# Four graph layers on one core: list keys by ScalarE and PE, and layer 0's row arithmetic moved between engines

## Chip, cores and metric

The kernel runs on one core of one Trainium2 chip. The metric is the device time of one execution in microseconds; lower is better. A profiled execution also gives a span, from its first to its last instruction, and the times inside it.

## What is computed

The input x holds 8 batches of 2048 nodes with 64 features, and adj a sparse 2048 x 2048 matrix of 0 and 1, the same for all batches. Four attention layers follow each other, each on the normalized and rectified rows, each added to x:

```python
h = jnp.maximum(_layernorm(x), 0.0); x = x + L0(h, adj)      # softmax(h h^T / 8, masked by adj) h
h = jnp.maximum(_layernorm(x), 0.0); x = x + L1(h, adj, W, a) # additive attention, elu
h = jnp.maximum(_layernorm(x), 0.0); x = x + L2(h, adj, ...)  # four heads, projection, second attention, layernorm
h = jnp.maximum(_layernorm(x), 0.0); x = x + L3(h, adj, W, a) # additive attention, relu
```

A node without neighbours takes the mean of all rows in layers 0, 1 and 3, since its masked softmax is uniform.

## The kernel before

**Layout.** Nodes lie in 16 tiles of 128 partitions; a row holds all batches, 8 x 64 = 512 float32 values (F). Attention is done edge by edge: for every tile the kernel makes lists of neighbour indices, gathers the neighbours' rows from a table in HBM into a ring of 26 slots in SBUF (`gather`, L260, one indirect DMA of POOL for each slot, 81 slots a layer), makes scores, weighs the rows and sums them on PE. A node's first few neighbours have slots of their own (`ROWS`); the rest of all nodes of a tile are packed into further slots (`PACKED`), which a selection matrix assigns to their nodes. Tile 0 holds the nodes with most neighbours and has 17 slots, the others 2 to 8.

**Stages.** `pipeline` runs a list of stage functions over the 16 tiles, each stage one tile behind the one before, the later stages first in each turn. That is the order in which the program is written down. A scheduler then reorders the instructions of each engine; an engine executes its own in the order that results. The first `pipeline` (set-up) loads x (`xin_rows`), normalizes it (`norm_a`, `norm_b`, `pre_c`) and stores the rows in table 0 (`pre_d`, `store_rows`). The second makes the lists (`load_adj`, `lists`), gathers from table 0 (`take0`), makes scores and their exponentials (`first0`), weights and sums (`second`), divides and adds to x (`third0`, `add_store`), normalizes again and stores table 1. Layer 1's gathers need all of table 1 and its mean row, and so on through tables 2, 3 (which have no mean row) and 4; table 4 is stored in the second half of layer 2 (after the four heads).

**Set-up of weights.** Before all this SP issues some 20 small transfers (L147 to L195), PE and VectorE form `u1`, `u3` and `q2` from them (L161 to L183, eight narrow copies to `q2`), and POOL issues three broadcasts of 64 values (L199) and seven of zero rows (L138, L140).

**Lists.** `load_adj` loads 128 x 2048 int32 values (L620). `lists` turns them into keys with one VectorE instruction over 2048 columns (L627): N + 1 minus the column where there is an edge, else 0. Then `max` (L633) finds the eight largest keys in each of 8, 16 or 22 segments of columns, for tile 0 twice with `match_replace` (L635) between; from these candidates `max` and `match_replace` (L643, L645) sort out the list, and narrow steps (L648 to L709) make indices, masks and the selection matrix, with small products on PE (L662, L685, L697) and the banks `q` and `m` in PSUM.

**Norms.** `norm_a` sums x on VectorE (L277). In set-up it does not centre: VectorE makes minus the mean (L289), ScalarE squares in eight pieces with it as bias (L291), POOL makes the product of mean and scale (L302), and ScalarE normalizes and rectifies in eight pieces (L308). In layer 0 it centres: VectorE makes the mean (L281) and subtracts it (L284), and ScalarE squares 512 columns at once (L285). `norm_b` sums the squares on VectorE (L297).

**Layer 0's end.** `third0` divides the sum `y` in PSUM on VectorE (L481) and `add_store` adds x to it there (L489).

**Mean row.** `store_rows` adds each tile's rows to `acc` on POOL (L367, L369; for tables 0, 1 and 4). After the last tile PE sums over partitions (L372), VectorE copies a row of 512 (L375) and SP stores it (L376).

**Products and sums.** `weigh_sum` multiplies two gathered rows at a time by their weights on POOL (L390) and sums them on PE (L395). L438 selects query rows on PE, L355 makes layer 1's per-node terms and L806 is the division of the four heads on ScalarE, in pieces of 64 columns.

Of the kernel before, what the change touches and what calls it, by code (L numbers as in the profile page):

```python
# [8 lines left out]
F32 = mybir.dt.float32  # L9
F16 = mybir.dt.float16  # L10
# [6 lines left out]
P = 128  # L17
# [14 lines left out]
SEGS = [(24, 2), (16, 1)] + [(8, 1)] * 14  # L32
RING = 26
# [5 lines left out]
SPREAD = 3  # L39

# [7 lines left out]
def segments(n, count, least):  # L48

    ends, lo = [], 0  # L50
    for k in range(1, count + 1):
        hi = n * k * k // (count * count)
        if hi - lo >= least:
            ends.append((lo, hi))
            lo = hi
    if lo < n:
        ends[-1] = (ends[-1][0], n)
    return ends
# [3 lines left out]
def edge_stack(ctx: ExitStack, tc: tile.TileContext, x_in, adj, w1, w1t, a1, wh, wht, bh, wo, bo,  # L62
# [47 lines left out]
    acc = const.tile([P, F], F32, name="acc")  # L110
# [28 lines left out]
    for k in (2, 3):  # L139
        nc.gpsimd.dma_start(out=table[k][N:N + 1, :], in_=zrow[:, :F])  # L140


    def diag2(name, src):

        t = const.tile([P, P], F32, name=name)
        nc.gpsimd.memset(t, 0.0)
        nc.sync.dma_start(out=t[:D, :D], in_=src)  # L147
        nc.sync.dma_start(out=t[D:, D:], in_=src)
        return t

    with tc.tile_pool(name="setup", bufs=1) as sp, \
            tc.tile_pool(name="ps_w", bufs=2, space=bass.MemoryType.PSUM) as ps_w:
        def attend_weights(name, wt, a):

            w2 = sp.tile([D, 2, D], F32, name="w2", bufs=2)
            nc.sync.dma_start(out=w2[:, 0, :], in_=wt)
            nc.sync.dma_start(out=w2[:, 1, :], in_=wt)
            av = sp.tile([D, 2], F32, name="av", bufs=2)
            nc.sync.dma_start(out=av, in_=a)
            p = ps_w.tile([P, D], F32, name="p")  # L160
            nc.tensor.matmul(p[:, :2], w2.rearrange("j t i -> j (t i)"), av, start=True, stop=True)  # L161
            u = const.tile([P, 4], F32, name=name)
# [3 lines left out]
            return u  # L166

        wd1, wd3 = diag2("wd1", w1), diag2("wd3", w3)
        u1, u3 = attend_weights("u1", w1t, a1), attend_weights("u3", w3t, a3)


        q2 = const.tile([P, 2, H, D], F32, name="q2")
        nc.gpsimd.memset(q2, 0.0)
        wh2 = sp.tile([D, H, 2, D], F32, name="wh2")
        for t in range(2):
            nc.sync.dma_start(out=wh2[:, :, t, :], in_=wh.rearrange("h d c -> d h c"))
        for h in range(H):
            p = ps_w.tile([P, D], F32, name="p")
            nc.tensor.matmul(p, wh2[:, h].rearrange("d t c -> d (t c)"), wh2[:, h, 0, :],
                             start=True, stop=True)  # L180
            for t in range(2):
                half = slice(t * D, (t + 1) * D)
                nc.vector.tensor_copy(q2[half, t, h, :], p[half, :])  # L183
    whd = [const.tile([P, P], F32, name=f"whd{k}") for k in range(2)]
    for k in range(2):
        nc.gpsimd.memset(whd[k], 0.0)
        for t in range(2):
            nc.sync.dma_start(out=whd[k][t * D:(t + 1) * D, t * D:(t + 1) * D], in_=wht[2 * k + t])
    bhc = const.tile([P, 2], F32, name="bhc")
    for k in range(2):  # L190
        nc.sync.dma_start(out=bhc[:, k:k + 1], in_=bh[k * P:(k + 1) * P].rearrange("(p o) -> p o", o=1))
    bhl = const.tile([P, 2], F32, name="bhl")
    nc.vector.tensor_scalar(bhl, bhc, SLOPE, None, op0=OP.mult)
    wo_sb = const.tile([P, 2, D], F32, name="wo")
    nc.sync.dma_start(out=wo_sb, in_=wo.rearrange("(k p) d -> p k d", p=P))  # L195

    def row_bcast(name, src, n):
        t = const.tile([P, n], F32, name=name)
        nc.gpsimd.dma_start(out=t, in_=bass.AP(tensor=src.tensor, offset=src.offset,  # L199
                                               ap=[[0, P], [1, n]]))  # L200
        return t

    bo_b = row_bcast("bo_b", bo, D)
    gamma_b = row_bcast("gamma_b", gamma, D)
    beta_b = row_bcast("beta_b", beta, D)


# [11 lines left out]
    def pipeline(*stages):  # L219

        states = {}
        for n in range(NT + len(stages) - 1):
            for s in reversed(range(len(stages))):
                if 0 <= n - s < NT:
                    i = order[n - s]
                    stages[s](i, states.setdefault(i, {}))
# [47 lines left out]
    def norm_a(src, st, centre):  # L274
# [4 lines left out]
        if centre:  # L279
            mean = tiny(B)  # L280
            nc.vector.tensor_scalar(mean, s, INV_D, None, op0=OP.mult)  # L281
            st["less"] = None
            st["src"] = rows_pool[0].tile([P, F], F32, name="ln_xc", bufs=3)
            nc.vector.tensor_tensor(heads(st["src"]), heads(src), wide(mean), op=OP.subtract)  # L284
# [38 lines left out]
    def pre_c(u):  # L323
        def f(i, st):
            st["xh"] = rows_pool[0].tile([P, F + B], F32, name="xh", bufs=3)
            scaled(st["xh"], st, AF.Relu)
# [35 lines left out]
    def store_rows(k, i, xh, mean):  # L362
        cols = table[k].shape[1]
        nc.sync.dma_start(out=table[k][i * P:(i + 1) * P, :], in_=xh[:, :cols])
        if mean:
            if i == order[0]:
                nc.gpsimd.tensor_copy(acc, xh[:, :F])  # L367
            else:
                nc.gpsimd.tensor_tensor(acc, acc, xh[:, :F], op=OP.add)  # L369
            if i == order[-1]:  # L370
                p = ps_m.tile([P, F], F32, name="m")
                nc.tensor.matmul(p[:1, :], ones, acc, start=True, stop=True)  # L372
                mr = rows_pool[0].tile([1, F + B], F32, name="mr", bufs=1)
                nc.vector.memset(mr[:, F:], 0.0)
# [108 lines left out]
    def third0(i, st):  # L483
        divide(st, st["y"])
        add_store(i, st, st["y"], True)
# [967 lines left out]
```

## Time and profile before

| | us |
|---|---|
| median of three runs | 1628.55 |
| the three runs | 1628.55, 1629.81, 1625.19 |
| the profiled execution's own time | 1627.04 |
| its span | 1625.3 |
| VectorE busy | 1289.1 (79%) |
| PE busy | 1209.7 (74%) |
| POOL busy | 1015.0 (62%) |
| ScalarE busy | 771.0 (47%) |
| first gather of layer 0 starts | 109.5 |
| first gather of layer 1 starts | 400.0 |
| first gather of layer 3 (table 4) starts | 1463.4 |

In a group's line the columns are: line, engine, operation, output and inputs, shapes, count; then busy time in us and mean ns of one; then the idle time of the engine just before these instructions, and what ended it. In a table by stretches each engine has its busy us and the number of its instructions. In a timeline a line begins with the start and the duration in us. DVE is VectorE, ACT ScalarE, POOL GpSimd, SP the engine that issues most DMAs; PEld is the load of weights into PE.

### The profile page before, as it was taken

To read this page: it belongs to the slowest core of one execution; us is meant where nothing else is said; L and a number is where in the kernel's file an instruction comes from. 1 tells how busy PE (TensorE), PEld (TensorE's weight loads), DVE (VectorE), ACT (ScalarE), POOL (GpSimd) and SP (SyncE) were. 2 spreads that over 40 slices of the span, in tenths; PEclk is the share of its full clock that TensorE was granted. 3 is DMA by queue.
4 is the path that set the end of the run, shared out by engine and by line. 5 is a ranking of instruction groups with operands and counts; after the bars stand their busy time and mean duration, and the time that the engine had idled before them with its cause. 6 is when DMAs were issued, how large, how long until landed. Compare 5 with 4: busy or idle time off the path is not lost. (4 is left out here: it accounts for less than half of the span.)

```text
span 1625.3 us, 15664 instructions
## 1 busy us (share of the span) xinstructions
PE 1209.7 (74%) x3771; PEld 607.8 (37%) x3771; DVE 1289.1 (79%) x2594; ACT 771.0 (47%) x2522; POOL 1015.0 (62%) x823
## 2 busy tenths in 40 slices
PE   0024766876799983699987999999766878855997
PEld 0012243444454531234343344443333334423555
DVE  6978999994689996899999699871159979954677
ACT  5861323444377882456532455555426446760011
POOL 4345865664763006898689889898276686527550
PEclk9999787787899997799999999999967987857899
DMA  5545555453787448566265344400084453227771
GB/s 177 179 152 190 179 189 174 142 186 122 225 289 264 155 160 309 203 207 211 66 223 185 121 151 170 164 13 7 30 313 139 125 168 120 79 79 218 214 211 61
DMA packets 85786, 266.93 MB, mean 164 GB/s; under 512 B 14627, under 2 KB 14659, under 8 KB 75446
## 3 DMA queue, kind: packets, MB, share of 16 engines
q0 software_dynamic: 37328, 141.05, 28.0%
q1 hardware_dynamic: 48358, 124.79, 21.8%
q8 instruction: 32, 0.52, 0.1%
q14 instruction: 68, 0.56, 0.1%
HBM read 208.74 MB, written 57.05 MB: 164 GB/s over the span
## 5 line engine op out<-in xcount | busy, mean ns | idle before, releaser
L260 POOL DMA_INDIRECT g<-table,idx x405 | 396.3, 978 | 234.2 <-issue 135.2
L783 POOL TENSOR_TENSOR wh<-g,w 128x1024 f32<-128x1024 f32 x162 | 307.3, 1918 | 35.6 <-PE y L798 33.6
L395 PE MATMUL y<-wg,ident 128*128 128x512 f32 x392 | 240.9, 744 | 50.2 <-POOL wg L390 44.2
L390 POOL TENSOR_TENSOR wg<-g,w 128x1024 f32<-128x1024 f32 (+1 forms) x91 | 155.1, 1717 | 74.8 <-ACT w L446 44.6
L770 DVE TENSOR_REDUCE s<-prod 128x32 f32<-128x2048 f32 x81 | 183.8, 2285 | 20.3 <-ACT w L772 19.9
L798 PE MATMUL y<-wh,ident 128*128 128x512 f32 x320 | 155.7, 614 | 22.7 <-POOL wh L796 20.6
L395 PE MATMUL y<-wg,selt 128*128 128x512 f32 x256 | 138.6, 651 | 8.7 <-POOL wg L390 8.1
L395 PEld LDWEIGHTS y<-wg,ident 128*128 128x128 f32 x392 | 83.2, 232 | 136.3 <-issue 67.4
L798 PE MATMUL y<-wh,selt 128*128 128x512 f32 x256 | 125.1, 614 | 12.1 <-POOL wh L783 12.1
L806 ACT ACTIVATE yn<-y,rec 128x64 f32<-128x64 f32 x512 | 111.3, 367 | 30.4 <-PE y L798 29.7
L369 POOL TENSOR_TENSOR acc<-acc,xh 128x512 f32<-128x512 f32 x45 | 58.0, 1288 | 96.8 <-ACT xh L308 84.6
L766 DVE TENSOR_TENSOR prod<-q,g 128x2048 f32<-128x2048 f32 x49 | 111.4, 2274 | 3.6 <-ACT g L764 3.3
L390 DVE TENSOR_TENSOR wg<-g,tiny 128x1024 f32<-128x1024 f32 (+1 forms) x92 | 98.2, 1085 | 11.6 <-PE y L395 11.2
L452 DVE SCALAR_TENSOR_TENSOR zt<-m,bhc,att 128x512 f32<-128x512 f32 x64 | 47.1, 736 | 75.3 <-ACT att L451 75.3
L438 PE MATMUL q<-rows,sel 128*128 128x512 f32 x128 | 84.3, 762 | 17.6 <-DVE prod L440 9.2
L798 PEld LDWEIGHTS y<-wh,ident 128*128 128x128 f32 x320 | 59.6, 195 | 96.9 <-issue 62.6
L409 PEld LDWEIGHTS m<-w,selt 128*128 128x128 f32 x384 | 62.6, 211 | 88.4 <-issue 26.2
L308 ACT ACTIVATE xh<-x,ln_r 128x64 f32<-128x64 f32 x256 | 88.3, 428 | 14.6 <-POOL ln_r L302 13.6
L409 PE MATMUL m<-w,selt 128*128 128x8 f32 (+1 forms) x384 | 59.7, 258 | 44.9 <-ACT w L555 17.2
L764 ACT COPY g<-g 128x512 f32<-128x512 f32 x81 | 50.4, 622 | 86.5 <-DVE prod L766 77.4
L790 PE MATMUL y<-rows,ident 128*128 128x512 f32 x128 | 70.2, 634 | 18.7 <-DVE prod L766 13.6
L766 DVE TENSOR_TENSOR prod<-qe,g 128x2048 f32<-128x2048 f32 x32 | 72.9, 2279 | 12.9 <-DMA qe<-qtab,qidx 11.7
(208 smaller groups left out, 2515.9 us busy)
## 6 DMA issues: line engine op xcount, KB each, us to landing
qtab<-q SPq DMA_DIRECT2D x16, 1040.0 KB, 4.3
a<-in_adj_dram SPq DMA_DIRECT2D x16, 1024.0 KB, 7.0
q<-qtab SPq DMA_DIRECT2D x14, 1040.0 KB, 6.3
table<-xh SPq DMA_DIRECT2D x48, 256.0 KB, 2.2
rows<-table SPq DMA_DIRECT2D x48, 256.0 KB, 3.6
xs<-x SPq DMA_DIRECT2D x48, 256.0 KB, 2.4
x<-xs SPq DMA_DIRECT2D x48, 256.0 KB, 4.6
table<-xh SPq DMA_DIRECT2D x32, 260.0 KB, 2.0
```

The costliest lines, as they stand in the source:

```text
L260: g = nc.gpsimd.indirect_dma_start(out=ring[:, (held[i] + t) % RING, :cols], out_offset=None, in_=table[k][:, :], in_offset=bass.IndirectO ...
L308: nc.scalar.activation(dst[:, b * D:(b + 1) * D], st["src"][:, b * D:(b + 1) * D], func, bias=0.0 if st["less"] is None else r[:, 1, b:b + ...
L390: eng.tensor_tensor(wg[:, :m].rearrange("p t (b d) -> p t b d", b=B), g[:, :, :F].rearrange("p t (b d) -> p t b d", b=B), w[:, t0:t0 + m, ...
L395: nc.tensor.matmul(y, lhs(i, t), wg[:, t - t0, :], start=(t == 0 and own is None), stop=(t == n - 1))
L409: nc.tensor.matmul(p[:, :cols], selt(i, t), packed[:, t, :], start=(t == 0), stop=(t == T - 1))
L438: nc.tensor.matmul(qe, sel(i, t - K), q, start=True, stop=True)
L766: nc.vector.tensor_tensor(pr.rearrange("p (b h) d -> p b h d", h=H), q[:, :B * H * D].rearrange("p (b h d) -> p b h d", h=H, d=D), heads(g ...
L770: nc.vector.tensor_reduce(s[:, t - lo, :], pr, AX.X, OP.add)
L783: nc.gpsimd.tensor_tensor(wg, heads(row(i, t))[:, :, None, :].to_broadcast([P, B, 2, D]), w[:, :, 2 * k:2 * k + 2, None].to_broadcast([P, ...
L790: nc.tensor.matmul(st["ys"][j], ident, xb[:, 4 * j:4 * j + 4], start=True, stop=False)
L798: nc.tensor.matmul(st["ys"][j], lhs(i, t), wg[:, 4 * j:4 * j + 4], start=False, stop=(t == n - 1))
L806: nc.scalar.activation(yn[:, b, h, :], st["ys"][j][:, b, h, :], AF.Copy, scale=st["rec"][:, 4 * j + b, 2 * k + h:2 * k + h + 1])
```

## The change

- Keys: ScalarE turns the int32 values into signs in bf16, in two halves of 1024 columns. PE makes each 512 columns of keys in PSUM from two bf16 products: 4096 times the sign, and the key N + 1 minus the column from two rows of small numbers that POOL makes once. Segments now end at multiples of 512. `max` and `match_replace` work in PSUM, and a narrow VectorE pass takes 4096 off the candidates, with zero as the floor.
- Layer 0: ScalarE divides in eight pieces, POOL adds x, makes the mean and centres.
- Set-up: POOL makes mean and centring, ScalarE squares 512 columns at once, VectorE rectifies and scales in one instruction.
- Mean row: for each tile PE sums 128 columns at a time over partitions, VectorE adds the 128 x 4 result to `acc`; at the end PE transposes it and SP stores 4 x 128 values.
- Weights are loaded by a function that is called where the fourth tile's adjacency is loaded, behind the first x tiles. The eight narrow copies to `q2` become two.
- Layer 0's stages get other distances (`LAG0`: the lists run three tiles further ahead of the gathers), lists and loads are written first in each turn, and PSUM has two `q` banks and two key banks in place of three `q` banks and a bank for small values.

```diff
+LIFT = 4096.0
+AHEAD0, LAG0 = (1, 0), [0, 1, 4, 5, 6, 7, 8, 9, 10]
...
 def segments(n, count, least):
+    marks = [n * k * k // (count * count) for k in range(1, count + 1)]
+    for at in range(512, n, 512):
+        near = min(range(count), key=lambda k: abs(marks[k] - at))
+        marks[near] = at
...
-    def pipeline(*stages):
+    def pipeline(*stages, ahead=(), lag=None):
...
-    def norm_a(src, st, centre):
+    def norm_a(src, st, centre, eng=nc.vector):
...
         if centre:
-            mean = tiny(B)
-            nc.vector.tensor_scalar(mean, s, INV_D, None, op0=OP.mult)
+            mean = tiny(B) if eng is nc.vector else small.tile([P, B], F32, name="ln_m")
+            eng.tensor_scalar(mean, s, INV_D, None, op0=OP.mult)
...
-            nc.vector.tensor_tensor(heads(st["src"]), heads(src), wide(mean), op=OP.subtract)
+            eng.tensor_tensor(heads(st["src"]), heads(src), wide(mean), op=OP.subtract)
...
-    def pre_c(u):
+    def pre_c(u, eng=None):
...
-            scaled(st["xh"], st, AF.Relu)
+            if eng is None:
+                scaled(st["xh"], st, AF.Relu)
+            else:
+                eng.scalar_tensor_tensor(heads(st["xh"][:, :F]), heads(st["src"]), 0.0,
+                                         wide(st["rstd"][:, 0, :]), op0=OP.max, op1=OP.mult)
...
         if mean:
+            C = F // P
+            p = ps_m.tile([P, F], F32, name="m")
+            for c in range(C):
+                nc.tensor.matmul(p[:, c:c + 1], xh[:, c * P:(c + 1) * P], ones, start=True, stop=True)
             if i == order[0]:
-                nc.gpsimd.tensor_copy(acc, xh[:, :F])
+                nc.vector.tensor_copy(acc, p[:, :C])
             else:
-                nc.gpsimd.tensor_tensor(acc, acc, xh[:, :F], op=OP.add)
+                nc.vector.tensor_tensor(acc, p[:, :C], acc, op=OP.add)
             if i == order[-1]:
                 p = ps_m.tile([P, F], F32, name="m")
-                nc.tensor.matmul(p[:1, :], ones, acc, start=True, stop=True)
-                mr = rows_pool[0].tile([1, F + B], F32, name="mr", bufs=1)
-                nc.vector.memset(mr[:, F:], 0.0)
-                nc.vector.tensor_copy(mr[:, :F], p[:1, :])
-                nc.sync.dma_start(out=table[k][N:N + 1, :], in_=mr[:, :cols])
+                nc.tensor.transpose(p[:C, :P], acc, ident)
+                mr = rows_pool[0].tile([C, P], F32, name="mr", bufs=1)
+                nc.vector.tensor_copy(mr, p[:C, :P])
+                nc.sync.dma_start(out=table[k][N, :F].rearrange("(c p) -> c p", p=P), in_=mr)
...
     def third0(i, st):
-        divide(st, st["y"])
-        add_store(i, st, st["y"], True)
+        y = rows_pool[0].tile([P, F], F32, name="att")
+        for b in range(B):
+            nc.scalar.activation(y[:, b * D:(b + 1) * D], st["y"][:, b * D:(b + 1) * D], AF.Copy,
+                                 scale=st["rec"][:, b:b + 1])
+        x = st["x"]
+        nc.gpsimd.tensor_tensor(x, x, y, op=OP.add)
+        nc.sync.dma_start(out=xs[i], in_=x)
+        norm_a(x, st, True, nc.gpsimd)
...
             def load_adj(i, st):
-                st["a"] = pool.tile([P, N], I32, name="a")
-                nc.sync.dma_start(out=st["a"], in_=adj[i * P:(i + 1) * P, :])
+                if i == order[WAT]:
+                    weights_in(pool)
+                st["e"] = pool.tile([P, N], BF16, name="e")
+                for c in range(0, N, N // 2):
+                    a = pool.tile([P, N // 2], I32, name="a")
+                    nc.sync.dma_start(out=a, in_=adj[i * P:(i + 1) * P, c:c + N // 2])
+                    nc.scalar.activation(st["e"][:, c:c + N // 2], a, AF.Sign)
...
-                key = st["a"].bitcast(F32)
-                nc.vector.scalar_tensor_tensor(key, st["a"], 0.0, keyrow, op0=OP.is_gt, op1=OP.mult)
...
+                for c in range(0, N, F):
+                    key = ps_k.tile([P, F], F32, name="k")
+                    nc.tensor.matmul(key, lift, st["e"][:, c:c + F], start=True, stop=False)
+                    nc.tensor.matmul(key, every, keys[:, c:c + F], start=False, stop=True)
...
+                ends = c1.rearrange("p s r k -> p (s r k)")
+                nc.vector.tensor_scalar(ends, ends, LIFT, 0.0, op0=OP.subtract, op1=OP.max)
...
-            pipeline(xin_rows, lambda i, st: norm_a(st["x"], st, False), pre_b, pre_c(None), pre_d(0, None))
+            pipeline(xin_rows, lambda i, st: norm_a(st["x"], st, True, nc.gpsimd), pre_b,
+                     pre_c(None, nc.vector), pre_d(0, None))
             pipeline(load_adj, lists, take0, both(first0, xin_rows), second, third0, pre_b, pre_c(u1),
-                     pre_d(1, u1))
+                     pre_d(1, u1), ahead=AHEAD0, lag=LAG0)
```

`weights_in` issues the transfers, memsets, products and copies that stood at the program's start, and the three broadcasts of POOL.

## Prediction

> **What bounds the kernel now.** I read the busy time by stage first: the share over the whole span hides that only the first quarter is changed. The stages are cut at three places of POOL's timeline: the first landed x (16.6 us), the first gather of layer 0 (109.5) and the first gather of layer 1 (400.0).
>
> ```profile
> core 0: us, PE busy (x) PEld busy (x) DVE busy (x) ACT busy (x) POOL busy (x), PEclk, DMA share, GB/s
> 0.00:16.60 16.60, 3.47 (x12) 2.91 (x12) 3.12 (x16) 1.28 (x1) 11.02 (x35) 1.00 0.37 63
> 16.60:109.50 92.90, 3.50 (x9) 1.62 (x9) 78.09 (x260) 79.71 (x298) 29.58 (x33) 1.00 0.52 179
> 109.50:400.00 290.50, 199.15 (x607) 107.72 (x607) 260.58 (x795) 106.53 (x377) 184.27 (x143) 0.83 0.52 172
> ```
>
> VectorE works 78 of 93 us in set-up, where ScalarE is as full (80), and 261 of 290 us in layer 0; between 140 and 360 us most stretches of 10 us show it at 8.4 to 10.0. So VectorE bounds the first 400 us, and its work there is what an edit can shorten. Next, the groups of 16.6 to 400 us by shape, to see what the edited lines cost:
>
> ```profile
> L627 DVE SCALAR_TENSOR_TENSOR a<-a,keyrow 128x2048 f32<-128x2048 int32 x16 | 38.2, 2390 | 7.7 <-DMA a<-in_adj_dram 7.7
> ...
> L481 DVE TENSOR_TENSOR y<-y,rec 128x512 f32<-128x512 f32 x16 | 11.0, 689 | 0.5 <-PE y L395 0.5
> L489 DVE SCALAR_TENSOR_TENSOR x<-y,x 128x512 f32<-128x512 f32 x16 | 10.9, 681 | 0.1
> L284 DVE TENSOR_TENSOR ln_xc<-x,tiny 128x512 f32<-128x512 f32 x16 | 10.8, 676 | 0.1
> ```
>
> The last column is small in all of these: VectorE hardly waits before them. The same groups on POOL, which will take up work:
>
> ```profile
> L260 POOL DMA_INDIRECT g<-table,idx x82 | 87.5, 1067 | 51.5 <-issue 31.9 <-DVE idx L708 7.2 <-DVE junk L659 4.7
> L390 POOL TENSOR_TENSOR wg<-g,w 128x1024 f32<-128x1024 f32 x36 | 68.5, 1906 | 34.6 <-ACT w L446 16.8 <-PE y L395 9.1 <-issue 6.5
> L369 POOL TENSOR_TENSOR acc<-acc,xh 128x512 f32<-128x512 f32 x30 | 38.9, 1298 | 51.0 <-ACT xh L308 42.4 <-ACT xh L358 2.7 <-DVE c L645 1.6
> L390 POOL TENSOR_TENSOR wg<-g,w 128x512 f32<-128x512 f32 x9 | 9.4, 1044 | 5.4 <-ACT w L446 5.4
> ```
>
> Last, the timeline at the end of layer 0, where the mean row is what layer 1 waits for:
>
> ```profile
> 391.70 1.27 POOL L369 TENSOR_TENSOR acc<-acc,xh 128x512 f32<-128x512 f32 x1 [1.75 <-ACT xh L308]
> ...
> 395.23 1.86 PE L372 MATMUL m<-acc,ones 128*1 128x512 f32 x2
> ...
> 397.13 0.68 DVE L375 COPY mr<-m 1x512 f32<-1x512 f32 x1 [8.82 <-PE m L372]
> 397.84 0.24 SPq L376 DMA_DIRECT2D table<-mr  x1
> 399.97 0.98 POOL L260 DMA_INDIRECT g<-table,idx  x1 [7.01 <-issue]
> ```
>
> **What the Trainium skill says.** "GPSIMD Engine Reference", section 1, has its SBUF interface shared with VectorE, with contention against VectorE instructions that have two SBUF inputs or a 2-port mode. The trace agrees: a pair of 128x8 products on POOL (L302, usually 0.20 us each) takes 2.33 us at 45.59 us, while L627 runs on VectorE. Section 4.1 calls two-input elementwise work about 2x slower there; here 128x512 takes 1.27 us (L369) against 0.68 (L489). "TensorE: Matmul & The Clock Gate", part 1, halves the clock after an idle window; the table above shows 0.83 granted in layer 0.
>
> **The change, part by part.** Durations are of the profiled execution: span 1625.3 us, its own time 1627.0, 1.5 below the median of 1628.55.
>
> *Off VectorE:* L627 38.2; division, addition, centring 11.0 + 10.9 + 10.8; the means L281 and L289 2.5 + 4.2; set-up's copies L183 1.8 less 0.7; two mean-row copies 1.4. Together 80 us. *Onto VectorE:* set-up's rectify-and-scale as one 128x512 instruction per tile, 16 x 0.68 = 10.9 (price of L489); removing the lift from the candidates, 16 narrow passes, 3.5 by their widths; 32 mean-row additions of 128x4 at 0.15 (as L666), 4.8; and 194 searches and replacements that now read PSUM. The nearest rows, one element from PSUM and from SBUF, are 144 ns (L666) and 133 (L663): 194 x 11 = 2 us; "VectorE: DVE Perf Modes", errata section, puts 62 cycles between the two, at its 0.96 GHz 65 ns, 12.6 us; I take 3. Sum 22. Net: 341.8 - 80 + 22 = 284 us of VectorE work. It is on the path, as VectorE bounds.
>
> *Earlier start:* x is now issued first, weights later. VectorE starts at about 5 us (one issue of 0.6, landing 2 to 4) and not at 16.6. The 20 weight transfers of 0.33 to 0.6 us each now stand on SP among list loads and ahead of the seventh x; six loaded x and the lists cover their 11 us, which is the price if they don't. The three on POOL (1.9 us) stand between the first means and the first centring; POOL's memsets, iotas (two key rows, some 1.9 each like L598) and nine zero-row issues take 15.5 us before that.
>
> *ScalarE:* loses L291 (32.5) and set-up's L308 (43.5); gains 16 squares of 0.627 (10.0), 32 signs of 128x1024 and layer 0's division as 128 pieces at 111.3/512 = 0.217 each (L806), 28. A sign has no row: "ScalarE: Activation LUTs" prices 186 + 0.833 N ns, 1.04 us; the slope of L679 (364 ns at 128 columns, 692 at 512) gives 1.13. I take 1.04, 33 us in all, 36 at the upper end. About even at 187 us; covered by VectorE and POOL.
>
> *PE:* gains 128 bf16 key products of 512 columns. A float32 one is two instructions, 0.43 us each at full clock; bf16 lies between 0.22 ("VectorE: DVE Perf Modes", 6 + N cycles at 2.4 GHz) and 0.43: I take 0.25 with weights, 32 us (28 to 55). The mean rows are eight small instructions per tile as at L355, some 0.9 us, 16 tiles a table. Layer 0's PE need at full clock is 143 us now (81 sums of 2 x 0.43, 70; 32 selections 28; the small ones 45) and 176 then (72 late keys 19, mean rows 14): inside the window found below, but no longer slack.
>
> *POOL:* loses L369 and L367 (41 us in these stages). Set-up gains 16 centrings of 1.04 (L390) to 1.27 (L369), taken as 1.16, and 16 means of 0.2: 22 us. Layer 0 gains the same and 16 additions of 1.27: 42 us.
>
> *New waits:* division on ScalarE, addition, mean and centring on POOL form a loop through POOL's queue, where each add waits for ScalarE and each mean for VectorE, with gathers and products queued behind. The key products wait on PE behind sums that wait for POOL, with two key banks and two instead of three q banks; lists run three tiles further ahead to cover it.
>
> **The sum for layer 1's first gather.** The built order of the changed kernel puts 26 gathers, tile 0's 17 slots among them, before POOL's first product; the last need tile 0's list. Ahead of its end stand on VectorE, counted in that order: norms 16 x (0.60 + 0.60 + 0.60 + 0.15) = 31 us; tile 0's own list 34 (44 searches and 22 replacements by segment 12.5, 31 passes over 352 candidates at 0.5, small steps); five other lists and one search 33. That is 98, and 5% for stalls in small steps, since the same count of the kernel before gives 323 where 341.8 is busy: 103 us. From 5 us at 93% that ends at 116 us. POOL then has 55 gathers at 0.95 + 0.30 spacing (69), products 68.5 + 9.4 (78) and 42: 189 us. VectorE has 284 - 103 = 181. POOL is now the longer. Layer 2 (700 to 1100 us), where POOL is 347.5 us busy of 400, shows the share a leading POOL reaches: 87%. 189/0.87 = 217, so 333. From the last centring to the gather about 10 us (square 0.6, ln_q 0.6, ln and exp 0.5, xh 2.0, transposes and copy 1.2, L355 0.9, copies 0.3, store 2.0, issues the rest): 343 instead of 400.0, so 57 saved.
>
> *Layer 3:* the stage that makes its table (1200 to 1463 us) drops 20 us of POOL adds, next to VectorE's 227 of 263 us, for 14 us of PE. At the end the mean row no longer follows 1.86 us of products and a 0.68 us copy; table rows stored at 1459.1, landing 2.0 later, are late next: 2 to 3 of the gap to 1463.4 go. I take 3 for the stage, zero to 6. The other stages keep their order nearly whole: 0. Total 1627.0 - 60 = 1567 in the profiled scale, about 1568 against the median; I write 1567.
>
> **Rivals.** *Both queues fill:* if VectorE and POOL overlap as VectorE alone did before (97%), 112 + 189/0.97 + 10 = 317: 83 + 3 saved, 1541. For: L627's blocking of POOL is gone, some 11 us. Against: two full engines wait on each other. *Coupling takes it:* POOL reaches only what it had from 172 to 392 us, 144 busy + 16 of issue gaps of 220, 73%: 116 + 259 + 10 = 385, 1609. For: waits of 2 to 5 us before products in the trace. Against: VectorE, which caused them, has slack. *Slower:* the POOL loop. 48 added waits per layer (add, mean, centre, 16 tiles); the sum without idleness is 116 + 189 + 10 = 315, so it decides from (403 - 315)/48 = 1.8 us each. At 2.3 us, near the waits of 2.8 seen before L369, it is 425 and, less 3, 1649. Against: the order puts other work between. *The change does nothing:* freed time is only waited through, 1627.
>
> **How the numbers follow.** Forecast 0.55, both full 0.15, coupling 0.17, POOL loop 0.10, nothing 0.03. Faster by over 0.3% (about what a measurement of this kernel can tell from no change) is the first three, less a corner of coupling: 0.86; same 0.03; slower 0.11. The range 1535 to 1617 leaves out the slower case, the unchanged one and the outer parts of coupling and of both full; the forecast's own is 1545 to 1590.
>
> **What would show it.** First gather of layer 0 near 60 us; POOL's 26th gather at 105 to 125; layer 1's first at 320 to 365; VectorE's sum to there near 284; L627's 38 us gone; table-end gaps shorter by 2 to 3 us. It is wrong if POOL's idle time before the moved adds and centrings passes 1.8 us each, if PE is busy throughout layer 0, or if later stages move by over 10 us.

## The result, and the profile after

The changed kernel takes 1599.64 us (median of 4 runs, 1596.62 to 1602.38) against 1626.87 for the kernel before beside it: ratio 0.983, 95% interval 0.980 to 0.986, 27 us less. Repeated on another chip the ratio was 0.982 (0.978 to 0.985). The forecast was 60 us less. The profiled execution took 1597.0 us, its span is 1595.3, so the profiles differ by 30 us (1625.3 before).

Busy time of the changed kernel by stage, cut at layer 0's first gather, at POOL's first product, after the last centring and at layer 1's first gather:

```profile
core 0: us, PE busy (x) PEld busy (x) DVE busy (x) ACT busy (x) POOL busy (x), PEclk, DMA share, GB/s
0.00:77.50 77.50, 46.28 (x164) 31.80 (x165) 53.35 (x196) 29.93 (x68) 37.55 (x73) 1.00 0.74 227
77.50:139.30 61.80, 38.76 (x112) 18.50 (x111) 55.43 (x289) 19.00 (x40) 24.67 (x26) 0.92 0.60 193
139.30:353.70 214.40, 189.46 (x694) 104.73 (x694) 185.00 (x542) 127.57 (x473) 170.22 (x148) 0.86 0.54 173
353.70:367.30 13.60, 9.68 (x44) 8.72 (x43) 1.45 (x5) 4.58 (x17) 0.02 (x2) 0.50 0.21 78
```

Layer 0's first gather comes 32 us earlier than before (77.5 against 109.5), but POOL's first product does not: 139.3 against 133.7. From there to layer 1's first gather it is 228 us instead of 266, and this is the gain that is left: 367.3 against 400.0. After that 1228 us follow, 3 more than before. Two places of VectorE's and POOL's timelines in set-up show what became of the early start (in brackets: idle time before, and what ended it):

```profile
8.35 0.17 DVE L621 TENSOR_SCALAR nn<-pe 128x16 f32<-128x16 f32 x1
21.85 0.83 DVE L191 TENSOR_SCALAR bhl<-bhc 128x2 f32<-128x2 f32 x1 [13.34 <-DMA bhc<-in_bh_dram]
22.59 0.67 DVE L267 TENSOR_REDUCE ln_s<-x 128x8 f32<-128x512 f32 x1
```

```profile
101.30 0.95 POOL L250 DMA_INDIRECT g<-table,idx  x1 [0.30 <-issue]
129.60 0.94 POOL L250 DMA_INDIRECT g<-table,idx  x1 [27.34 <-DVE mbb L692]
```

A 128x2 step for layer 2's bias stands eighth among VectorE's instructions, and its transfer (bhc) stands on SP behind list loads: VectorE's bulk begins at 21.9 us. POOL waits 27 us for the rest of tile 0's list, and eight gathers at 1.25 us follow before its first product.

The end of layer 0 in the changed kernel:

```profile
362.28 1.84 PE L363 MATMUL m<-ones,xh 128*128 128x1 f32 x8
...
364.16 0.16 DVE L367 TENSOR_TENSOR acc<-m,acc 128x4 f32<-128x4 f32 x1 [5.05 <-PE m L363]
...
364.88 0.28 DVE L372 COPY mr<-m 4x128 f32<-4x128 f32 x1 [0.56 <-PE m L370]
365.19 0.27 SPq L373 DMA_DIRECT2D table<-mr  x1
367.29 1.03 POOL L250 DMA_INDIRECT g<-table,idx  x1 [13.58 <-DMA table<-mr]
```

The mean row is still last. Its eight products take 1.84 us here, where the clock on record is 0.50, and 0.95 to 1.04 in the dense stretch from 320 to 345 us, where it is 1.00.

Next, the stretch of VectorE's bulk, from its start to where the last scores are done, before (first fence) and after:

```profile
16.60:378.00 361.40, 187.42 (x559) 100.02 (x560) 329.64 (x1036) 174.70 (x631) 207.35 (x170) 0.88 0.53 178
```

```profile
21.80:340.00 318.20, 260.95 (x903) 146.02 (x904) 287.00 (x1008) 159.09 (x524) 204.36 (x191) 0.89 0.59 190
```

VectorE is as full as before (90% against 91%), with 43 us less of work in 43 us less of time. POOL is at 64%. What has changed is PE: 52% before, 82% after.

### The profile page after: what moved, and what is told of

It is laid out like the page before. It is cut to its first block, busy times and chain, and to the rows that moved or that the text cites. A ratio compares the mean times of both kernels' runs of the same rounds, so it can differ in the third digit from the quotient of the medians.

```text
span 1595.3 us, 16704 instructions
## 1 busy us (share of the span) xinstructions
PE 1293.1 (81%) x4280; PEld 672.1 (42%) x4280; DVE 1245.6 (78%) x2569; ACT 762.7 (48%) x2443; POOL 1002.1 (63%) x844
## 4 chain that ended last, share of the span: by engine, by line
PE 34%; DVE 17%; POOL 10%; ACT 10%; issue 9%; DMA 7%; SPq 0%; POOLq 0%; DVEq 0%; ACTq 0%
PE y L392 9%; PE y L820 9%; POOL g L250 5%; DMA g<-table,idx 4%; DVE prod L788 3%; DVE s L792 3%; POOL wh L805 3%; ACT yn L828 2%; DMA rows<-table 2%; ACT xh L298 2%; PE y L812 2%; PE m L869 2%; PE m L857 2%; PE q L435 2%; DVE wg L387 2%
## 5 line engine op out<-in xcount | busy, mean ns | idle before, releaser
L250 POOL DMA_INDIRECT g<-table,idx x405 | 386.8, 955 | 290.2 <-issue 111.1
L392 PE MATMUL y<-wg,ident 128*128 128x512 f32 x392 | 225.7, 705 | 19.5 <-POOL wg L387 11.7
L392 PE MATMUL y<-wg,selt 128*128 128x512 f32 x256 | 131.0, 621 | 2.3 <-POOL wg L387 2.3
L392 PEld LDWEIGHTS y<-wg,ident 128*128 128x128 f32 x392 | 79.5, 222 | 97.6 <-issue 62.1
L435 PE MATMUL q<-rows,sel 128*128 128x512 f32 x128 | 80.8, 730 | 9.1 <-DVE prod L437 7.4
L333 PE MATMUL q<-q,xt 128*128 128x512 f32 x128 | 67.3, 635 | 18.3 <-DVE prod L335 10.4
L363 PE MATMUL m<-ones,xh 128*128 128x1 f32 x384 | 68.8, 302 | 10.4 <-DVE idx L729 3.5
```

The lines of the kernel that those rows point to most:

```text
L250: g = nc.gpsimd.indirect_dma_start(out=ring[:, (held[i] + t) % RING, :cols], out_offset=None, in_=table[k][:, :], in_offset=bass.IndirectO ...
L363: nc.tensor.matmul(p[:, c:c + 1], xh[:, c * P:(c + 1) * P], ones, start=True, stop=True)
L392: nc.tensor.matmul(y, lhs(i, t), wg[:, t - t0, :], start=(t == 0 and own is None), stop=(t == n - 1))
L435: nc.tensor.matmul(qe, sel(i, t - K), q, start=True, stop=True)
```

## The experiments

Theory 1, the blocked start: the early list work is what counts, and the wait for bhc takes it away. Theory 2: when VectorE starts matters little, since tile 0's list and what follows set the rest. Theory 3: the mean row costs more on PE than on POOL. Theory 4, formed after the first runs: POOL's start-up work holds the front. Ratios are to the kernel before on the same chip: on some chips it takes 1627 us, on others 1673 to 1675. The difference lies behind layer 1's first gather. This is layer 1's stage of the changed kernel in the first profile and in its repetition:

```profile
367.30:587.90 220.60, 183.62 (x662) 98.19 (x662) 177.32 (x342) 146.64 (x426) 80.20 (x97) 0.93 0.63 211
```

```profile
368.10:610.30 242.20, 185.70 (x662) 99.23 (x662) 177.25 (x342) 146.67 (x426) 80.16 (x98) 0.89 0.58 192
```

The same work on each engine takes 22 us longer where the DMA engines move 192 GB/s instead of 211; up to 367 us the two profiles agree within 1 us. So stages are compared only up to layer 1's first gather, and times as ratios. 0.001 of the time before is 1.6 us.

One thing limits most of these runs: the scheduler orders each edited program anew. How much of the changed kernel's order is left was counted in the traces, up to layer 1's first gather, as the longest sequence that both have in common. With the bias first, with table 4's mean row on POOL and in the first two runs on the end of the tables, at least 1021 of VectorE's 1029 instructions keep their order. In the other edited runs it is 569 to 940, so they weigh their edit together with a new order. Layer 1's first gather comes at 362 to 368.5 us in the first group and at 369 to 405 in the second: the order may itself be worth several us, and no run tries it apart.

In the line after each run: ratio (interval); layer 0's first gather, POOL's first product, layer 1's first gather in us.

**The changed kernel again**, with no edit.

> The changed kernel as it is, for a profile on the same chip as the three runs with added work. All theories: ratio 0.983 within 0.003; first product at 139, layer 1's first gather at 367 within 5 us.

Measured: 0.9816 (0.9781 to 0.9850); 77.5, 140.2, 368.2. It repeats.

**The bias first.** The two transfers of bhc and the step on them at the head of the program:

```
-            nc.sync.dma_start(out=bhc[:, k:k + 1], ...)      # in weights_in
-        nc.vector.tensor_scalar(bhl, bhc, SLOPE, None, op0=OP.mult)
+    for k in range(2):                                       # ahead of weights_in
+        nc.sync.dma_start(out=bhc[:, k:k + 1], ...)
+    nc.vector.tensor_scalar(bhl, bhc, SLOPE, None, op0=OP.mult)
```

> The changed kernel with the two bias transfers issued first and the 128x2 product of bhl behind them, so that no wait of 13.3 us on VectorE is left; all else in its order. Theory 1 (the early list work on VectorE sets the time, and the wait for bhc at 8.5 to 21.9 us takes it away): VectorE works through 10 to 20 us, the last of the first 26 gathers ends near 129 instead of 139.3, layer 1's first gather comes near 357 instead of 367.3, time near 1588 (10 less than the changed kernel). Theory 2 (the lists' first rows, x behind them on SP and tile 0's chain of small steps set it, whenever VectorE starts): the idle time only moves to waits for x, keys or PE, layer 1's first gather within 3 us of 367, time 1595 to 1600.

Measured: 0.9819 (0.9795 to 0.9844); 75.2, 137.9, 365.8. The 13 us wait is gone and 1.5 to 2.4 us come of it. Nearly all else keeps its order (1026 of VectorE's 1029 instructions). VectorE's timeline of this run shows the next wait in its place:

```profile
16.97 0.69 DVE L269 TENSOR_REDUCE ln_s<-x 128x8 f32<-128x512 f32 x1 [8.60 <-POOL ln_m L273]
```

The first means stand on POOL behind its memsets, key rows and issues. The blocked start is real, but as the explanation of the missing time it falls.

**POOL's start-up too.** The bias first, and the nine zero-row and three broadcast transfers issued by ScalarE:

```
-        nc.gpsimd.dma_start(out=table[k][N + 1:N + 2, :], in_=zrow[:, :table[k].shape[1]])
+        nc.scalar.dma_start(out=table[k][N + 1:N + 2, :], in_=zrow[:, :table[k].shape[1]])
```

> The kernel with the bias first, and besides POOL's nine zero-row transfers and three broadcast transfers (together 6.9 us of POOL's first 22) issued by ScalarE, so that the key rows and the first centring come some 6 us earlier. Theory 4 (what ends the start-up is POOL: its memsets, iotas and issues stand ahead of the first centring at 19.8 us and of the keys, and VectorE has little to do before): the first gather of layer 0 comes near 70 instead of 75.2, tile 0's list at 124 instead of 128.2, the ratio to before 0.979. Theory 2 (tile 0's list and what follows set it): 129 at the earliest, ratio as that of the run with the bias first, 0.982.

Measured: 0.9859 (0.9825 to 0.9894); 71.0, 138.8, 383.5. The first gather moves as expected; the first product does not move at all, and the end of layer 0 comes later. VectorE is busy for only 10.4 of the 20 us from 80 to 100, with gaps of 3.4 and 3.2 us, ahead of a weights' copy and a key search, whose cause the trace doesn't name. Theory 4 finds no support; it isn't refuted, as the order is new and the twelve transfers now stand in ScalarE's queue.

**Tile 0 first** in the order of making:

```
-MAKING = [15, 14, 13, 0, 12, 11, 10, 1, 9, 2, 8, 3, 7, 4, 6, 5]
+MAKING = [0, 15, 14, 13, 12, 11, 10, 1, 9, 2, 8, 3, 7, 4, 6, 5]
```

> The changed kernel with tile 0, whose list of 17 slots takes VectorE 34 us, first in the order in which lists and table rows are made, not fourth; all else as changed. If POOL's wait of 27 us for tile 0's list at 102 to 130 us (and its eight gathers, 9.7 us, behind it) is what took the gain, products start near 110 instead of 139 and layer 1's first gather comes 15 to 20 us earlier: ratio 0.972. If VectorE's total work sets the time, whatever its order, or POOL's stretch only grows: ratio within 0.003 of the changed kernel's 0.983.

Measured: 0.9847 (0.9817 to 0.9877); 77.2, 133.5, 377.4.

**No lists ahead:**

```
-                     pre_d(1, u1), ahead=AHEAD0, lag=LAG0)
+                     pre_d(1, u1))
```

> The changed kernel with layer 0's stages one turn apart in the old order (no lists ahead). If lists that run three tiles ahead keep the first scores, and so POOL's first product, waiting until 139 us, the first product comes near 105 and the time falls by up to 15 us: ratio 0.974. If the lead covers the key products' waits on PE behind sums, as the prediction had it, VectorE waits for keys in layer 0: ratio 0.990 to 1.000.

Measured: 0.9832 (0.9788 to 0.9875); 77.3, 88.8, 379.4. The first product comes 50 us earlier and the kernel is no faster. With the last two runs this speaks against POOL's late first product as what the end of layer 0 hangs on. It doesn't show it, since these edits change the order of all engines too, and this one takes away the lists' lead.

**Weights first**, `weights_in(pool)` called ahead of both pipelines:

> The changed kernel with its weights' transfers and small products called ahead of the two pipelines, as the kernel before had them; all else as changed. If the later weights are what brings the earlier start (as the prediction had it, 11 us of transfers on SP), x comes some 10 us later and the time rises by about 10, to 1610. Theory 1: the changed kernel loses those 10 us anyway, to bhl's wait and to x behind weights and lists; the time stays within 4 us of the changed kernel's, near 1600, or falls a little below it.

Measured: 0.9866 (0.9845 to 0.9888); 83.4, 144.6, 383.8. It lies between the two: 6 us later at the first gather and some 7 us in the time. The later weights, with the order that comes with them, are worth that.

**Work added in layer 0, read by nobody**, to see which engine holds it. One edit each, behind the added x (VectorE, POOL) and in the mean row of table 1 (PE):

```
+        nc.vector.tensor_reduce(spare, heads(x), AX.X, OP.add)         # 16 x 0.68 us
+        nc.gpsimd.tensor_tensor(spare, x, x, op=OP.add)                # 16 x 1.27 us
+                    nc.tensor.matmul(p[:, C + c:C + c + 1], xh[:, c * P:(c + 1) * P], ones, ...)
```

> The changed kernel with one more reduction of 128x512 per tile on VectorE in layer 0, behind the added x: 16 x 0.68 = 10.9 us more of its work, read by nobody. If VectorE still bounds the first stages (it starts its bulk at 22 us, has 295 us of work and a drain of some 22 us behind its last bulk), the time rises by 10 to 12 us, ratio 0.990. If POOL bounds layer 0, as the prediction had it, by less than 3: ratio 0.983 to 0.985.

Measured: 0.9866 (0.9830 to 0.9902); 75.9, 139.7, 387.1. Against the repetition, which ran on the same chip, it is 8 us for 10.9, and all four times lie above all four of that run. Layer 1's first gather comes 19 us later; the same code behind it then takes 1265.9 us, against 1276.9 in the repetition, and why is open.

> The changed kernel with one more POOL addition of 128x512 per tile in layer 0, behind the added x: 16 x 1.27 = 20 us more of its work, read by nobody. If POOL bounds layer 0 (the prediction's sum: 189 us of work at 87%), the time rises by 20 us or more, ratio 0.996. If VectorE bounds it, by less than 5: ratio 0.983 to 0.986. If both are coupled through their waits, in between.

Measured: 0.9819 (0.9783 to 0.9854); 77.8, 141.2, 374.6. On the same chip again, there is no loss in the time for 20 us of POOL work (6 us at layer 1's first gather in this one profile).

> The changed kernel with the small products of table 1's mean row done twice: 64 more products of 128x1 and weights, 0.95 to 1.84 us per tile, 15 to 29 us of PE's time in layer 0, read by nobody. If PE has slack in layer 0 (189 of 214 us busy, at 0.86 of the clock), the time rises by no more than the tail's 1.8 us: ratio 0.983 to 0.985. If PE's in-order queue bounds it, by 15 us and more: ratio 0.993.

Measured: 0.9896 (0.9852 to 0.9940); 76.7, 140.1, 379.8. Some 10 us, with a wide interval that just touches the changed kernel's; all four times lie above those of the repetition. So the runs suggest that POOL has room and that VectorE and PE have little. They don't show it, for the order is new in each: with the POOL work, for instance, VectorE keeps 905 of 1029 instructions in order, PE 888 of 1010 and ScalarE 491 of 597, though nothing was added to these.

**Less VectorE work**: the lift removed by ScalarE.

```
-                nc.vector.tensor_scalar(ends, ends, LIFT, 0.0, op0=OP.subtract, op1=OP.max)
+                nc.scalar.activation(ends, ends, AF.Relu, bias=unlift)
```

> The changed kernel with the removal of the lift (16 steps of 128x64 to 128x352, 8.9 us of VectorE, of which 6 are waiting inside the instruction) on ScalarE, as one rectify with a bias. If VectorE's work sets the first 340 us, they shorten by 6 to 10 us: ratio 0.977. If the round trip through ScalarE's queue costs each list its own wait: ratio 0.982 to 0.988.

Measured: 0.9809 (0.9783 to 0.9834); 76.9, 140.6, 369.1. VectorE has 275 us of work from 21.8 to 340 instead of 287, and next to nothing comes of it. Either VectorE does not hold the stretch alone, or the way through ScalarE's queue and the new order (745 of 1029 kept) cost as much as was saved; this run can't tell.

**Parts undone.** Layer 0's division, addition, mean and centring back on VectorE (`divide(st, st["y"])` and `add_store(i, st, st["y"], True)` in `third0`):

> The changed kernel with layer 0's division, addition, mean and centring back on VectorE (32.6 us there, 42 us off POOL, 28 off ScalarE). The prediction's sum (POOL leads layer 0 with 189 us, VectorE has 181): the balance turns, VectorE has 214 and POOL 147, the stretch after the first product grows by some 10 us, ratio 0.989. Rival (the move was what made POOL the longer and gained nothing): ratio 0.978 to 0.983.

Measured: 0.9939 (0.9910 to 0.9969); 76.8, 140.3, 383.2. This part, with its order, is worth some 19 us.

Set-up's norm back on ScalarE:

```
-            pipeline(xin_rows, lambda i, st: norm_a(st["x"], st, True, nc.gpsimd), pre_b,
-                     pre_c(None, nc.vector), pre_d(0, None))
+            pipeline(xin_rows, lambda i, st: norm_a(st["x"], st, False), pre_b, pre_c(None), pre_d(0, None))
```

> The changed kernel with set-up's norm as before: means folded into ScalarE's squares (32.5 us) and its rectify (43.5 us), nothing of it on POOL, 11.3 us of rectify off VectorE. If set-up is held by VectorE and the wait for x and lists, ScalarE's 76 us fit beside them and the time stays within 5 us: ratio 0.980 to 0.986. If ScalarE's signs (33 us over lists) wait behind these, set-up ends near 105 us as before and the time rises by 15 to 25 us: ratio 0.993 to 0.999.

Measured: 0.9893 (0.9869 to 0.9918); 107.2, 150.6, 378.8. Set-up ends 30 us later, as before the change, but the kernel loses only some 11 us.

The mean rows back on POOL, in tables 0, 1 and 4, then in table 4 alone:

```
+            if i == order[0]:
+                nc.gpsimd.tensor_copy(wide_acc, xh[:, :F])
+            else:
+                nc.gpsimd.tensor_tensor(wide_acc, wide_acc, xh[:, :F], op=OP.add)
```

> The changed kernel with the mean row of tables 0, 1 and 4 added on POOL and closed by one PE product of 128x1 by 128x512, as before; all else as changed. Theory 3 (the small fp32 products on PE, 1.84 us a tile at half clock, cost more than POOL's 1.26 us adds): layer 0's first gather comes some 3 us earlier, the tail of layer 0 shortens by 3, layer 3's stage by 4; time near 1590. Rival (POOL leads layer 0, so 16 adds of 1.26 us lengthen it): 139 to 354 us grows by about 20 us, against 7 gained at the ends; time near 1612.

Measured: 0.9954 (0.9937 to 0.9971); 86.8, 151.7, 394.4.

> The changed kernel with the mean row of table 4 alone added on POOL as before. Theory 3: layer 3's stage loses the 4.6 us by which it grew, time near 1595 (4 to 5 less than the changed kernel). Rival (the growth there comes from elsewhere, such as the two transfers into the table's last row, or is spread by chance of the order): within 2 us of the changed kernel, 1598 to 1602.

Measured: 0.9800 (0.9776 to 0.9823); 77.5, 141.2, 368.5. The first costs some 20 us, so theory 3 finds no support for the whole of the mean rows. Want of POOL time is hardly the reason in layer 0, as the run with added POOL work suggests; in set-up, where 9 of the 20 us are lost, no such run was made. These adds wait for a finished row, with gathers and products queued behind, which fits but was not tried apart. In table 4 alone it makes no difference that can be told.

All three parts undone, which leaves keys by sign and PE, later weights and lists ahead:

> The change cut down to its keys by ScalarE's sign and PE, the later weights and the lists three turns ahead: set-up's norm back on ScalarE with its rectify, layer 0's division, addition, mean and centring on VectorE, the mean rows on POOL as before. VectorE's law (its work over 0.90 of the time between its start and its end): 295 + 33 in layer 0 and, in set-up, +4 for the means, less 11.3 for the rectify, 4.5 for mean rows, so 316 us of work against 295, some 23 us later than the changed kernel, ratio 0.997. If POOL bounds the changed kernel's layer 0, giving it back 62 us of adds and centrings shortens it: ratio 0.975.

Measured: 1.0062 (1.0041 to 1.0083); 111.3, 168.2, 405.4. Alone they make the kernel 10 us slower, although VectorE has 23 us less to do up to layer 1 (319 against 342). Which of the three does it, or whether the order does, was not tried apart. The three parts are worth some 50 us one by one and some 40 together, so they overlap.

**The end of the tables.** The mean row of the last five tiles of tables 1 and 4 by VectorE, from the transposed tile that is there anyway:

```
+            late = k in (1, 4) and i in order[-5:]
+            if late:
...
+                nc.vector.tensor_reduce(col, xt, AX.X, OP.add)
+                nc.vector.scalar_tensor_tensor(acc, col, 1.0 / N, acc, op0=OP.mult, op1=OP.add)
```

> The changed kernel, but the mean row of the last five tiles of tables 1 and 4 is summed by VectorE from the transposed row tile that exists already (one reduction of 0.68 us and one 128x4 step), not by PE. If PE's small products at half clock hold up the end of layer 0 (4.8 us a tile for transposes, u and mean row, of which the mean row is 1.84), the stretch from VectorE's last bulk to layer 1's first gather shrinks from 27 to 22 us and layer 3's end by 1 to 3: 5 to 8 us less than the changed kernel, ratio 0.978. If the end waits for ScalarE's and POOL's steps anyway: ratio 0.981 to 0.984.

Measured: 0.9745 (0.9721 to 0.9768); 76.5, 140.0, 365.0. This is the one edit that pays, by 12 to 14 us, more than expected, and the order is kept (1024 of VectorE's 1029 instructions, all 970 that PE has left). The end of layer 0 in it:

```profile
359.68 0.69 DVE L364 TENSOR_REDUCE mcol<-xt 128x4 f32<-128x512 f32 x1 [2.98 <-ACT xt L307]
...
359.70 1.87 PE L349 MATMUL m<-u,xt 128*128 128x4 f32 x8 [0.68 <-ACT xt L307]
...
361.44 0.37 PE L376 MATMUL m<-ident,acc 128*4 128x128 f32 x1
...
362.28 0.29 SPq L379 DMA_DIRECT2D table<-mr  x1
365.04 1.03 POOL L250 DMA_INDIRECT g<-table,idx  x1 [11.15 <-DMA table<-mr]
```

From the last row (358.5 us) to the gather it is 6.5 us, where the changed kernel has 9.5 (357.8 to 367.3); at layer 3's end 6.5 against 8.0. These chains give 4.5 us of the 12 to 14; where the rest comes from was not found.

The same with layer 0's division, addition and centring of its last three tiles on VectorE, and then with the lift on ScalarE besides:

> The kernel with the last five tiles' mean rows on VectorE, and besides layer 0's division, addition, mean and centring of its last three tiles on VectorE, which idles from 340 to 367 us. If the chain of one tile through ScalarE and POOL (1.7 + 1.3 + 0.7 + 0.2 + 1.0 and their hand-overs) is late next at the end of layer 0, 2 to 4 us more go: ratio 0.972. If PE's transposes and u at half clock are (3 us a tile), nothing more goes: ratio 0.9745 within 0.002.

Measured: 0.9756 (0.9724 to 0.9787), 1586.25 us where before takes 1627.12; 79.3, 141.0, 362.2. Nothing more in the time.

> The last kernel with the removal of the lift on ScalarE besides. The run with that alone gave no gain that can be told from none (0.981 against 0.982 to 0.983), though VectorE's work fell by some 9 us: no gain here either, ratio as the last kernel's within 0.003. If the freed VectorE time only showed once the end of layer 0 is shorter: 5 us less, 0.969.

Measured: 0.9797 (0.9766 to 0.9829); 78.8, 141.3, 371.4. No better, if anything worse; the order is new again (743 of 1029 kept).

## Why the prediction was half right

The direction and most prices held: sign 1.053 us (1.04 forecast), POOL's centring 1.05 (1.16) and mean 0.23 to 0.30 (0.2), its addition 1.27 (1.27), VectorE's rectify 0.71 (0.68). The step that failed is "The sum for layer 1's first gather", in the terms below, and the one for layer 3. In short: VectorE began its bulk at 21.9 us and not at 5, eight gathers were left out, and PE, which the prediction held to be covered, came to twice its price:

- *POOL's 26th gather at 116.* It ended at 139.3, 23.3 later. The count of VectorE's work ahead of it was right (99.3 us by 129.6, forecast 103). VectorE was idle for 30.3 us instead of 13: beyond six short steps it did not "start at about 5 us", as the bias step held it (13.3 us; with that gone, POOL's start-up), and x came late in seven waits, 8.6 us. And the forecast let the stretch end with tile 0's list, leaving out the eight gathers behind it, 9.7 us.
- *"POOL is now the longer."* Its stretch took 214.4 us (forecast 217) and POOL was 87% full in it (170 us and 55 spacings of 0.30), just as put down. Yet 20 us of added POOL work cost nothing in the time, so that the number may have come out right by luck: the runs don't bear out the reason. The 87% was read in layer 2 between 700 and 1100 us, where PE is busy for 374 us and VectorE for 356, both more than POOL's 347.5; that stage did not show a leading POOL. The first product's time, on which this stretch was hung, could be moved by 50 us with no gain either.
- *PE, "inside the window".* The key products were priced at 0.25 us, the mean rows at 0.9 us a tile. Both come in two sizes. At 1.00 on the clock record a key product is busy for 0.38 to 0.39 us and starts 0.32 after the last (203.00, 203.31, 203.63, 203.95), and a mean row takes 0.95 to 1.04; at 0.50 it is 0.58 to 0.61, 0.54 apart, and 1.84. Ahead of 126 us, where the trace has no clock record (below), lie 68 of the 128 key products, at 0.58 to 0.63 us each, and all of set-up's mean rows, at 1.8 a tile (56 products in 12.63 us from 61.04):

```profile
74.05 0.60 PE L646 MATMUL k<-keys,every 33*128 33x512 bf16 x1
```

```profile
203.31 0.39 PE L646 MATMUL k<-keys,every 33*128 33x512 bf16 x1
```

  The groups of PE up to layer 1's first gather:

```profile
L363 PE MATMUL m<-ones,xh 128*128 128x1 f32 x256 | 49.6, 318 | 8.9 <-DVE idx L729 3.5 <-DVE ell L669 3.0 <-DVE xh L319 1.5
...
L646 PE MATMUL k<-keys,every 33*128 33x512 bf16 x64 | 32.8, 516 | 4.2 <-POOL keys L603 4.2
L645 PE MATMUL k<-e,lift 128*128 128x512 bf16 x64 | 32.5, 511 | 32.0 <-DVE c L652 16.9 <-ACT e L634 11.9 <-ACT ln_r L290 1.7
```

  That is 115 us busy, against 60 in the forecast (32 for keys, 28 for mean rows of two tables), with sums and selections queued behind them. One of the prediction's own signs of being wrong, a PE that is busy throughout layer 0, nearly came true: from 139.3 to 353.7 us PE is busy for 189 of 214.
- *The tail and layer 3.* From the last centring to the gather it took 13.6 us instead of 10, for the 1.84 us and PE's queue before it. The rest of the kernel took 2.7 us more instead of saving 3; identical code varies by up to 11 us between profiles on one chip there, so this term is not settled.

23.3 - 2.6 + 3.6 + 5.7 is the missing 30 us of the profiled scale. This accounts for it, but it isn't a list of causes: taking the bias wait out of the first term gave under 3 us. What is shown, with the order kept, is that the bias wait is worth that little, and that taking PE's mean-row products off the last five tiles of two tables is worth 12 to 14 us. That VectorE and PE hold the first 340 us together is the reading that fits best (more work on either costs, 20 us more on POOL do not), but it is inferred from runs whose order differs. The cause of most of the missing time stays open. VectorE's sum was 295 us, not 284; 5.4 of the 11 are the lift's removal, whose steps are held while POOL multiplies (below).

The rivals: "both queues fill" did not happen. "Coupling" is near in the time (1609) and not in its place, as it had POOL at 73%. The POOL loop, which would have ended slower, did not form. POOL's waits from 139.3 to 353.7 us (line, what ended it, us in total, times, longest):

```profile
POOL wg L387 <- ACT w L443: 9.8, 5, 4.4
POOL x L486 <- ACT att L483: 7.4, 3, 2.7
```

13 of the 16 additions show no such wait. "Does nothing" falls with the result.

## What to carry to other kernels

When work is lifted off the bound, price what is added on every in-order queue, short instructions and low clock included: here VectorE lost 43 us of work in its stretch and PE gained 74. A start that is pulled forward pays only up to the next thing that the pipeline waits for; look for it before counting the microseconds, and move a tiny step with a late transfer out of the head of a queue in any case. At the end of a stage, where here the clock was 0.50 and engines idled, a small product can stand on the path though it cost half as much in the middle. And where a scheduler orders the program, compare the order of the instructions before calling a run with added or removed work a test of that work.

## What the runs showed that was not expected

Short VectorE steps with one tensor input, from SBUF to SBUF and two or more columns wide, are held for as long as POOL's two-input product runs. Timelines of the changed kernel:

```profile
145.51 3.30 DVE L676 TENSOR_SCALAR mba<-ell 128x2 f32<-128x2 f32 x1
```

```profile
145.88 2.90 POOL L387 TENSOR_TENSOR wg<-g,w 128x1024 f32<-128x1024 f32 x2
```

```profile
254.27 0.14 DVE L676 TENSOR_SCALAR mba<-ell 128x1 f32<-128x1 f32 x1
```

The 128x2 step takes 0.16 us at 133.05 us, where POOL runs no product; the one shown takes 3.30 and ends at 148.81, with POOL's two products at 148.78. Up to layer 1's first gather ten such steps start while a POOL product runs that has at least 0.25 us to go. All ten end within 0.06 us of the end of a POOL product, after 0.4 to 3.7 us. The kernel before has 13 of them, and all are held in the same way. Steps one column wide are not held: eleven start under the same condition and take 0.13 to 0.15 us, like the third line above, at which POOL's addition runs on until 254.84. Nor are steps of the same kind with a PSUM side, which never exceed 0.17 us (L692) and 0.23 (L690). The Trainium skill has both halves of this: "GPSIMD Engine Reference", section 1, has the SBUF interface shared with VectorE instructions in a 2-port mode, and "VectorE: DVE Perf Modes", section "Mode 2×_2P", lets a single-source step use both read ports. The trace agrees for steps of two or more columns, and gives the price: the lift's removal came to 8.9 us where 3.5 were forecast.

PE's products run at half speed in set-up, although the tables give 1.00 as its clock there. The trace's clock records begin only at 126.1 us (at 148.1 before the change), and the 1.00 ahead of that stands for no record. From there on the spacing follows the record: mean-row products start 0.112 us apart in the median where it is 1.00 and 0.213 where it is 0.50, and in set-up the median is 0.213 again. So a clock of 1.00 at the start of a profile has to be checked against the spacing of like instructions. "TensorE: Matmul & The Clock Gate", part 1, ties half speed to an array that has been idle, which fits set-up, with PE busy for 46 of 77.5 us; no run here tries it.
